# Splitting depthwise convolutions between TensorE and VectorE, and products with C between GpSimd and VectorE, in a four-layer image kernel on one core

## The chip, the core and the metric

The kernel runs on one core of a Trainium2 chip. The core has five engines that run side by side, each through its own queue of instructions in order: TensorE (PE, matrix products into the PSUM memory), VectorE (DVE, elementwise work and scans), ScalarE (ACT, functions such as exp, and copies), GpSimd (POOL, elementwise work in the SBUF memory) and SyncE (SP, which here issues DMA transfers). Engines wait for each other by semaphores. A wait at the head of a queue holds up everything behind it.

The metric is the time of one execution on the device in microseconds (us); lower is better.

## The reference

The input is eight images of 64 channels and 64 x 64 pixels in float32. Four layers follow each other:

- Layer 0: 1x1 convolution, self-attention over all 4096 pixels, a depthwise 3x3 convolution, another 1x1 convolution, added to the input.
- Layer 1: two blocks of window attention (8 x 8 pixels, 8 heads) with their MLPs.
- Layer 2: a 3x3 filter whose weights depend on place and channel, then a 1x9 convolution.
- Layer 3: a state-space scan over the pixels in four directions, and then a module that mixes four resolutions (SAFM).

Cut to what the change touches:

```python
# layer 0, after the attention; layer 3, before the scan; layer 3, at the end:
y = depthwise_conv_3x3(x, w)           # nine taps, one weight per channel and tap

# layer 3, the scan: 128 channels, 16 states, 4 directions, 4096 pixels
def step(h, inp):
    u_t, dt_t, B_t, C_t = inp
    h = h * jnp.exp(dt_t[..., None] * A) + dt_t[..., None] * B_t[:, :, None, :] * u_t[..., None]
    return (h, jnp.einsum('bkcn,bkn->bkc', h, C_t))

# layer 3, SAFM: four groups of 16 channels, pooled by 1, 2, 4 and 8
s = _dwconv3(max_pool(parts[i], 2**i), mfr_w[i], mfr_b[i])     # then repeated back to 64 x 64
out = einsum('bchw,oc->bohw', concatenate(outs), aggr_w) + aggr_b
return gelu(out) * x
```

## The kernel before, in words

Images go in pairs: 64 channels of two images fill the 128 partitions. A pair's 4096 pixels are cut into eight chunks of 512 columns (`NCH`, `CH`), one bank of PSUM each.

`tile_kernel` runs the *front* of pair 0 alone: layers 0 to 2 and the sources of the scan. Then, for each pair p, `scans` runs the scan of pair p, and beside it other work as a Python generator: the *back* of pair p - 1 (the end of layer 3 and the output) and then the front of pair p + 1. The last pair's scan has only backs beside it. Each piece of such work yields a number, its cost in the planner's units, and `scans` advances the generator after each step of the scan so that the work ends with it. The emitted program then passes a scheduler that orders the instructions of each engine. The costs that are yielded are the same before and after the change.

A scan runs through 64 units a pair (2 images, 4 directions, 8 chunks), and each unit through 8 *steps* of two states: 512 steps a pair, 2048 in all. The partitions hold 64 channels times two states. A step of `scans` works like this:

- `fetch`: two DMAs on SP's queue spread the rows of B and C to all partitions.
- `products` (L1809): GpSimd multiplies B with dt*u for both halves, 1024 columns, into `v`, which has eight buffers.
- `step`: for each half, ScalarE writes exp(dt*A) into a PSUM bank `dad` (L1831), VectorE scans (L1834), and ScalarE keeps the last column in `carries` (L1842). Then the result is multiplied by C, into `v` again (L1845, L1848).
- `sums` (L1860): TensorE adds `v` up in the PSUM bank `yd`, two or three steps later.

Who multiplies by C is decided by `own`, the number of halves that VectorE takes. During the full attention (`dense`) and for the last two images `own` is 1, and 2 in every fourth step. In all other steps it is 0 and 1 in turn. With 0, both scans write to `h` in SBUF, one copy on ScalarE keeps both carries, and one GpSimd instruction of 1024 columns multiplies both halves (L1845). With 1, the second scan overwrites its PSUM bank and VectorE multiplies it, while GpSimd multiplies the first half.

A depthwise convolution of one chunk is `taps_sum`: nine products on TensorE with diagonal matrices of the tap's weights (`spread_taps`), added in one bank (L1275), or the first n of these and the others as multiply-adds on VectorE into the same bank (L1277). Three places use it: `cacc` in layer 0 (8 chunks a pair), `xacc` in `scan_sources` (8 chunks for each image) and `pa` in `back` (8 chunks a pair). In the first two, n is 5 while the front runs alone (`self.alone`) and 9 beside a scan. In `back`, unless it runs alone at the very end, the taps are taken with the aggregation matrix scaled by the tap's weight, so that convolution and aggregation are one sum of nine products; three products for the coarser resolutions follow (L1979), and the bias is made once by a small product (`pmb`, `ab`). Alone at the end, `back` does all nine taps on VectorE (L1264, L1266, tile `sacc`), copies the result to `S`, and multiplies it with the aggregation matrix.

Of the kernel before, what the change touches and what calls it, by code (L numbers as in the profile page):

```python
# [9 lines left out]
F32 = mybir.dt.float32  # L10
AF = mybir.ActivationFunctionType
ALU = mybir.AluOpType
# [3 lines left out]
B, C, HH, WW = 8, 64, 64, 64  # L16
# [1143 lines left out]
class _Direct:  # L1160
# [127 lines left out]
    def layer0(self, p):  # L1288


        nc, tc, w, net, half = self.nc, self.tc, self.w, self.net, self.HALF
        X = self.flat("X")
        nc.sync.dma_start(X, self.net.x[2 * p : 2 * p + 2].rearrange("b c h w -> (b c) (h w)"))
        att = self.padded("att")
        VT = self.flat("VT").rearrange("p (t c) -> p t c", c=P)

        def at(rows, t):
            return X[rows, t * P : (t + 1) * P]

        with self.work("w0") as wk:  # L1300
            for g in range(8):
                pv = self.bank("pval", (P, 4, P))
                nc.tensor.matmul(pv, lhsT=net.ones[0:1, :], rhs=net.b1row.rearrange("o a c -> o (a c)").unsqueeze(1).to_broadcast([1, 4, P]), start=True, stop=False)
                for j in range(4):
                    nc.tensor.matmul(pv[:, j, :], lhsT=at(slice(0, P), 4 * g + j), rhs=net.w1bd, start=False, stop=(j == 3))
                nc.scalar.activation(VT[:, 4 * g : 4 * g + 4, :], pv, AF.Relu)
                yield 3

            parts = wk.tile([P, 2, 32, NCH], F32, name="parts", tag="parts", bufs=1)
            self.dense = 1  # L1310
            for jc in range(NCH):
                po = self.total("po")

                def weigh(t, es):
                    for im in range(2):
                        nc.tensor.matmul(  # L1316
                            po[half[im]], lhsT=VT[:, t, half[im]], rhs=es[im], start=(t == 0), stop=(t == 31)
                        )

                last = None  # L1320
                for t in range(32):
                    ss = [self.bank(f"s{im}") for im in range(2)]
                    for im in range(2):
                        nc.tensor.matmul(  # L1324
                            ss[im], lhsT=at(half[im], t), rhs=X[half[im], jc * CH : (jc + 1) * CH], start=True, stop=True
                        )
                    es = []
                    for im in range(2):
                        e = wk.tile([P, CH], F32, name="e", tag="e", bufs=5)
                        nc.scalar.activation(  # L1330
                            e, ss[im], AF.Exp, scale=C**-0.5, accum_out=parts[:, im, t, jc : jc + 1]
                        )
                        es.append(e)
                    if last is not None:
                        weigh(*last)
                    last = (t, es)
                    yield 5.8
                weigh(*last)
                nc.vector.tensor_copy(self.rows(att, jc), self.img(po))

            self.dense = 0
            sums = net.sums[:, p]
            nc.vector.tensor_reduce(sums, parts, AX.X, ALU.add)
            rec = wk.tile([P, 2, 32], F32, name="rec", tag="rec", bufs=1)
            nc.vector.reciprocal(rec, sums)
            for g in range(8):
                pr = self.bank("prec")
                for j in range(4):
                    for im in range(2):
                        nc.tensor.matmul(  # L1350
                            pr[half[im], j * P : (j + 1) * P],
                            lhsT=rec[:, im, 4 * g + j : 4 * g + j + 1].to_broadcast([P, 64]),
                            rhs=w["ident"],
                            start=True,
                            stop=True,
                        )
                d = self.rows(att, g)
                nc.vector.tensor_tensor(d, d, self.img(pr), ALU.mult)
                yield 3
        with self.work("w0b") as wk:  # L1360
            diag = self.spread_taps(wk, w["dw2"])
            for c in range(NCH):
                acc = self.bank("cacc", (P, 8, 64))
                yield from self.taps_sum(acc, diag, att, 8 * c, 1.56, wt=w["dw2"], n=5 if self.alone else TAPS)
                cv = wk.tile([P, 8, 64], F32, name="cv", tag="cv")
                nc.scalar.activation(cv, acc, AF.Relu, scale=net.bn23[:, 0:1], bias=net.bn23[:, 1:2])
                pw = self.bank("pw")
                nc.tensor.matmul(pw, lhsT=w["w3bd"], rhs=cv, start=True, stop=True)
                nc.scalar.activation(pw, pw, AF.Identity, scale=net.bn23[:, 2:3], bias=net.bn23[:, 3:4])
                x = X[:, c * CH : (c + 1) * CH]  # L1370
                nc.vector.tensor_tensor(x, x, pw, ALU.add)
                yield 2.25
        return X
# [271 lines left out]
    def scan_sources(self, p, X2):  # L1645
# [3 lines left out]
        with tc.tile_pool(name="w3", bufs=2) as wk:  # L1649
# [9 lines left out]
            for im in range(2):  # L1659
# [9 lines left out]
                XT = self.flat("XT").rearrange("p (w h) -> p h w", h=64)  # L1669
                for c in range(NCH):  # L1670
                    acc = self.bank("xacc", (P, 8, 64))
                    yield from self.taps_sum(acc, diag, pad, 8 * c, 1.5, wt=w["cw"], n=5 if self.alone else TAPS)
                    cv = wk.tile([P, 8, 64], F32, name="xcv", tag="xz")
                    nc.scalar.activation(cv, acc, AF.Silu, bias=w["cb"])
                    last = nc.scalar.activation(XT[:, 8 * c : 8 * c + 8, :], cv, AF.Copy)
                    nc.scalar.dma_start(xc[:, c * CH : (c + 1) * CH], cv.rearrange("p a b -> p (a b)"))
                    yield 1.4
# [133 lines left out]
    def step(self, i, st):  # L1811
# [5 lines left out]


        n0 = 2 * (i % 8)
        own = 1 + (i % 4 == 3) if u["image"] >= B - 2 or self.dense else i % 2  # L1820
        rev = k >= 2

        def along(t):
            return t[:, ::-1] if rev else t

        h = wk.tile([P, 2 - i % 2, TD], F32, name="hd", tag=f"h{i % 2}", bufs=2)
        hs = []
        for j in range(2):
            n = n0 + j
            da = self.bank("dad", (P, TD), "da")  # L1830
            nc.scalar.activation(da, u["du"][:, j, 0], AF.Exp, scale=net.As[:, k, n : n + 1])  # L1831
            first = 0.0 if at == 0 else self.carries[:, n : n + 1]
            to = da if j >= 2 - own else h[:, j]
            nc.vector.tensor_tensor_scan(along(to), along(da), along(v[:, j]), first, ALU.mult, ALU.add)  # L1834
            hs.append(to)
            if at < NTD - 1 and (own or j):
                ends = h[:, :, 0] if rev else h[:, :, TD - 1]
                cs = self.carries[:, n0 : n0 + 2]
                if own:
                    ends = to[:, 0:1] if rev else to[:, TD - 1 : TD]  # L1840
                    cs = self.carries[:, n : n + 1]
                nc.scalar.activation(cs, ends, AF.Copy)  # L1842

        if own == 0:
            st["w"] = nc.gpsimd.tensor_tensor(v, h, self.twice(CC), ALU.mult)  # L1845
        for j in range(2 if own else 0):
            engine = nc.vector if j >= 2 - own else nc.gpsimd
            m = engine.tensor_tensor(v[:, j], hs[j], CC, ALU.mult)  # L1848
            st.setdefault("w", m)
# [32 lines left out]
    def back(self, p):  # L1882
# [27 lines left out]
        with tc.tile_pool(name="w5", bufs=1) as wk:  # L1910
            prev, n, ups = F, 64, []
            alone = p == B // 2 - 1
            for i in range(1, 4):
# [40 lines left out]
                ups.append(up)  # L1954
                prev = pool
                yield 7
            ab = w["aggr_b"]
            if not alone:
                near = self.spread_taps(wk, w["mw"][:, 0, :], w["agT"][:, 0, :])
                pm = self.bank("pmb")  # L1960
                nc.tensor.matmul(pm[:, 0:1], lhsT=w["agT"][:, 0, :], rhs=w["mb"][:, 0:1], start=True, stop=True)
                ab = wk.tile([P, 1], F32, name="ab", tag="ab")
                nc.vector.tensor_tensor(ab, pm[:, 0:1], w["aggr_b"], ALU.add)
            for c in range(NCH):
                cols = slice(c * CH, (c + 1) * CH)
                if alone:
# [4 lines left out]
                    pa = self.bank("pa", (P, 8, 64))  # L1971
                    nc.tensor.matmul(pa, lhsT=w["agT"][:, 0, :], rhs=S, start=True, stop=False)
                else:
                    pa = self.bank("pa", (P, 8, 64))
                    yield from self.taps_sum(pa, near, F, 8 * c, 1.5, stop=False)
                for i in range(1, 4):
                    k = 2**i
                    r = 8 // k
# [4 lines left out]
                        start=False,  # L1983
                        stop=(i == 3),
                    )
                last = nc.scalar.activation(pa, pa, AF.Gelu, bias=ab)
                nc.vector.tensor_tensor(pa, pa, self.rows(F, c), ALU.mult)
                nc.vector.tensor_tensor(X[:, cols], X[:, cols], pa.rearrange("p a b -> p (a b)"), ALU.add)
                nc.sync.dma_start(out[:, cols], X[:, cols])
# [53 lines left out]
```

## Time and profile before

Three runs took 11924.33, 11923.68 and 11909.1 us: the median is 11923.68 us. The profiled execution took 11912.44 us, with a span of 11910.6 us from its first to its last instruction.

| | PE | DVE | ACT | POOL |
|---|---|---|---|---|
| busy, us | 9941.2 | 7896.1 | 6958.5 | 7344.5 |
| share of the span | 83% | 66% | 58% | 62% |

The weight loads of TensorE (PEld, 3381.8 us) lie beside its products. TensorE's mean granted clock is 0.904 of full speed.

| from - to, us | what runs |
|---|---|
| 0 - 1561 | front of pair 0, alone |
| 1561 - 2595 | scan 0, beside the full attention of pair 1 |
| 2595 - 4158 | scan 0, beside the rest of the front of pair 1 |
| 4158 - 7008 | scan 1, beside the back of pair 0 and the front of pair 2 |
| 7008 - 9859 | scan 2, beside the back of pair 1 and the front of pair 3 |
| 9859 - 11911 | scan 3, beside the back of pair 2; the back of pair 3 at the end |

How to read the lines quoted below: times are in us, means in ns. L1848 is line 1848 of the kernel before; `vd<-hd,C` is what an instruction writes and reads; `128x512 f32` is 128 partitions times 512 columns of float32; x404 is how often. A float32 product appears as two rows of matmul. Matmuls are pipelined and the end of each is modelled, so the distance of their starts tells more than their length. "Idle before" is idle time of the engine before such instructions, with what ended most of it.

### The profile page before, as it was taken

The page shows a single profiled execution, that of the slowest core. Times are in us where ns is not written, and L with a number is a line of the kernel's source. Part 1 is how long each engine was busy: PE and PEld are TensorE (multiplying, and loading weights), DVE is VectorE, ACT ScalarE, POOL GpSimd, SP SyncE. Part 2 cuts the span into 40 slices and gives each one's busy share as a digit, 9 for nine tenths or more (in the row PEclk, how much of TensorE's full clock was granted, in tenths as well). Part 3 has the DMA queues.
Part 4 walks back from the last instruction along what each step waited for, and adds up shares of the span by engine and source line. Part 5 has one row for each costly group of instructions (what it writes and reads, how often), then busy time and mean ns, then how long its engine had stood idle before and what let it go on. Part 6 is the DMA issues. An engine that isn't in the chain of part 4 may idle for free. (4 is left out here: it accounts for less than half of the span.)

```text
span 11910.6 us, 161652 instructions
## 1 busy us (share of the span) xinstructions
PE 9941.2 (83%) x56180; PEld 3381.8 (28%) x56180; DVE 7896.1 (66%) x9071; ACT 6958.5 (58%) x16089; POOL 7344.5 (62%) x3799
## 2 busy tenths in 40 slices
PE   9987999998889779999888968999888886665565
PEld 2244332223332223223342313222333221111111
DVE  0033368876776475876766564777676648989998
ACT  5555367766664555775665554777566355555554
POOL 0000068876777574776756673777676658889994
PEclk9998999999999889999999979999999987786768
DMA  0000055554444453554433453555343346666663
GB/s 20 1 2 2 33 168 174 172 159 120 125 131 125 152 158 111 169 170 133 132 107 110 141 177 96 157 167 173 115 132 114 109 149 190 182 191 199 207 204 119
DMA packets 779774, 1577.05 MB, mean 132 GB/s; under 512 B 89280, under 2 KB 89408, under 8 KB 778176
## 3 DMA queue, kind: packets, MB, share of 16 engines
q1 hardware_dynamic: 736320, 1443.18, 39.9%
q10 hardware_dynamic: 42624, 123.44, 3.7%
q8 instruction: 444, 7.27, 0.3%
q14 instruction: 386, 3.16, 0.1%
HBM read 1197.16 MB, written 100.66 MB: 109 GB/s over the span
## 5 line engine op out<-in xcount | busy, mean ns | idle before, releaser
L1809 POOL TENSOR_TENSOR vd<-B,du 128x1024 f32<-128x1024 f32 x2048 | 4791.4, 2359 | 2982.0 <-DMA B<-rows 1733.3
L1860 PE MATMUL yd<-vd,pack 128*64 128x512 f32 x8192 | 2707.2, 690 | 637.7 <-POOL vd L1848 505.3
L1831 ACT ACTIVATE dad<-du,As 128x512 f32<-128x512 f32 x4096 | 2716.3, 682 | 708.8 <-DVE hd L1834 330.4
L1834 DVE TENSOR_TENSOR_SCAN hd<-dad,carry,vd 128x512 f32<-128x512 f32 x1874 | 2355.3, 1270 | 529.3 <-ACT dad L1831 400.0
L1834 DVE TENSOR_TENSOR_SCAN dad<-dad,carry,vd 128x512 f32<-128x512 f32 x1710 | 2153.0, 1277 | 186.4 <-ACT dad L1831 183.4
L1848 POOL TENSOR_TENSOR vd<-hd,C 128x512 f32<-128x512 f32 x1333 | 1698.1, 1278 | 651.6 <-DVE hd L1834 648.5
L1324 PE MATMUL s<-X 64*128 64x512 f32 x4096 | 1539.3, 646 | 75.4 <-ACT e L1330 66.8
L1330 ACT ACTIVATE e<-s 128x512 f32<-128x512 f32 x2048 | 1196.3, 588 | 483.7 <-PE s L1324 483.4
L1845 POOL TENSOR_TENSOR vd<-hd,C 128x1024 f32<-128x1024 f32 x404 | 952.2, 2357 | 794.2 <-issue 393.6
L1848 DVE TENSOR_TENSOR vd<-dad,C 128x512 f32<-128x512 f32 x1955 | 1296.6, 676 | 148.5 <-ACT carry L1842 115.1
L1860 PEld LDWEIGHTS yd<-vd,pack 128*64 128x64 f32 x8192 | 643.2, 151 | 2319.1 <-issue 1129.8
L1316 PE MATMUL po<-e,VT 128*64 128x512 f32 x4096 | 1259.4, 622 | 5.8 <-ACT e L1330 5.0
L1324 PEld LDWEIGHTS s<-X 64*128 64x128 f32 x4096 | 421.8, 186 | 1178.7 <-issue 832.5
L1842 ACT ACTIVATE carry<-dad 128x1 f32<-128x1 f32 x1707 | 286.4, 169 | 760.2 <-DVE dad L1834 656.7
L1842 ACT ACTIVATE carry<-hd 128x1 f32<-128x1 f32 (+1 forms) x1521 | 302.0, 200 | 625.2 <-DVE hd L1834 611.5
L1483 PE MATMUL w_av<-wide,vals 64*32 64x64 f32 x16384 | 490.7, 225 | 117.9 <-DVE w_oc L1512 74.6
L1316 PEld LDWEIGHTS po<-e,VT 128*64 128x64 f32 x4096 | 249.6, 135 | 833.7 <-issue 569.4
L1471 ACT ACTIVATE wide<-wide 128x512 f32<-128x512 f32 x512 | 310.7, 628 | 289.4 <-DVE wide L1470 289.2
L1483 PEld LDWEIGHTS w_av<-wide,vals 64*32 64x32 f32 x16384 | 402.7, 111 | 257.1 <-issue 138.1
L1834 DVE TENSOR_TENSOR_SCAN hd<-dad,vd 128x512 f32<-128x512 f32 x267 | 319.9, 1211 | 225.6 <-POOL vd L1809 189.0
L1494 PE MATMUL w_av<-wide,each 64*32 64x128 f32 x8192 | 463.2, 280 | 5.6 <-issue 5.4
L1243 PE MATMUL pv<-n_sq,pack 128*128 128x512 f32 x576 | 345.5, 683 | 143.9 <-ACT n_sq L1241 133.3
(259 smaller groups left out, 11257.1 us busy)
## 6 DMA issues: line engine op xcount, KB each, us to landing
B<-rows SPq DMA_DIRECT2D x2048, 256.0 KB, 3.6
C<-rows SPq DMA_DIRECT2D x2048, 256.0 KB, 3.5
du<-du SPq DMA_DIRECT2D x384, 512.0 KB, 5.6
du<-du ACTq DMA_DIRECT2D x128, 512.0 KB, 5.1
xs<-xt SPq DMA_DIRECT2D x128, 256.0 KB, 3.7
xs<-xc SPq DMA_DIRECT2D x128, 256.0 KB, 3.8
xc<-xcv ACTq DMA_DIRECT2D x64, 256.0 KB, 2.0
xt<-XT ACTq DMA_DIRECT2D x32, 512.0 KB, 4.8
```

Source lines behind the costliest of these rows:

```text
L1316: nc.tensor.matmul(po[half[im]], lhsT=VT[:, t, half[im]], rhs=es[im], start=(t == 0), stop=(t == 31))
L1324: nc.tensor.matmul(ss[im], lhsT=at(half[im], t), rhs=X[half[im], jc * CH : (jc + 1) * CH], start=True, stop=True)
L1330: nc.scalar.activation(e, ss[im], AF.Exp, scale=C**-0.5, accum_out=parts[:, im, t, jc : jc + 1])
L1483: nc.tensor.matmul(self.av[rows, 0, x % 4 + j], lhsT=net.vals[half[im], x + j, 4 * g + h], rhs=es[g][half[im], j, h], tile_position=(64 * ...
L1494: nc.tensor.matmul(self.av[rows, 1, x % 4 : x % 4 + 2], lhsT=net.each[half[im], 32 - HD - HD * h : 64 - HD - HD * h], rhs=es[g][half[im], ...
L1809: self.nc.gpsimd.tensor_tensor(v, self.twice(st["B"]), self.units[i // 8]["du"][:, :, 1], ALU.mult)
L1831: nc.scalar.activation(da, u["du"][:, j, 0], AF.Exp, scale=net.As[:, k, n : n + 1])
L1834: nc.vector.tensor_tensor_scan(along(to), along(da), along(v[:, j]), first, ALU.mult, ALU.add)
L1842: nc.scalar.activation(cs, ends, AF.Copy)
L1845: st["w"] = nc.gpsimd.tensor_tensor(v, h, self.twice(CC), ALU.mult)
L1848: m = engine.tensor_tensor(v[:, j], hs[j], CC, ALU.mult)
L1860: m = nc.tensor.matmul(u["y"][self.HALF[j]], lhsT=w["fold"], rhs=st["v"][:, j], start=(i % 8 == 0), stop=(i % 8 == 7))
```

## The change

It has three parts. The fronts that run beside a scan now split `cacc` and `xacc` as the front that runs alone does: five taps on TensorE, four on VectorE. In `step`, `own` is never 0: outside the attention and the last two images every step gives one half to GpSimd and one to VectorE, so the single instruction for both halves and the shared carry copy go away, and `h` is one tile of 512 columns with four buffers in place of two tags. In `back`, unless it runs alone, four taps are done by VectorE into `S`, a quarter of `big` with one buffer, to which the bias is added; one product with the aggregation matrix brings `S` into the sum, and five taps remain as products. The small bias product goes away.

```diff
@@ layer0
-                yield from self.taps_sum(acc, diag, att, 8 * c, 1.56, wt=w["dw2"], n=5 if self.alone else TAPS)
+                yield from self.taps_sum(acc, diag, att, 8 * c, 1.56, wt=w["dw2"], n=5)
@@ scan_sources
-                    yield from self.taps_sum(acc, diag, pad, 8 * c, 1.5, wt=w["cw"], n=5 if self.alone else TAPS)
+                    yield from self.taps_sum(acc, diag, pad, 8 * c, 1.5, wt=w["cw"], n=5)
@@ step
-        own = 1 + (i % 4 == 3) if u["image"] >= B - 2 or self.dense else i % 2
+        own = 1 + (i % 4 == 3 and (u["image"] >= B - 2 or self.dense))
...
-        h = wk.tile([P, 2 - i % 2, TD], F32, name="hd", tag=f"h{i % 2}", bufs=2)
+        h = wk.tile([P, TD], F32, name="hd", tag="h", bufs=4)
...
-            to = da if j >= 2 - own else h[:, j]
+            to = da if j >= 2 - own else h
...
-            if at < NTD - 1 and (own or j):
-                ends = h[:, :, 0] if rev else h[:, :, TD - 1]
-                cs = self.carries[:, n0 : n0 + 2]
-                if own:
-                    ends = to[:, 0:1] if rev else to[:, TD - 1 : TD]
-                    cs = self.carries[:, n : n + 1]
-                nc.scalar.activation(cs, ends, AF.Copy)
-
-        if own == 0:
-            st["w"] = nc.gpsimd.tensor_tensor(v, h, self.twice(CC), ALU.mult)
-        for j in range(2 if own else 0):
+            if at < NTD - 1:
+                ends = to[:, 0:1] if rev else to[:, TD - 1 : TD]
+                nc.scalar.activation(self.carries[:, n : n + 1], ends, AF.Copy)
+
+        for j in range(2):
@@ back
-            ab = w["aggr_b"]
             if not alone:
                 near = self.spread_taps(wk, w["mw"][:, 0, :], w["agT"][:, 0, :])
-                pm = self.bank("pmb")
-                nc.tensor.matmul(pm[:, 0:1], lhsT=w["agT"][:, 0, :], rhs=w["mb"][:, 0:1], start=True, stop=True)
-                ab = wk.tile([P, 1], F32, name="ab", tag="ab")
-                nc.vector.tensor_tensor(ab, pm[:, 0:1], w["aggr_b"], ALU.add)
...
+                    S = self.img(self.share(big, 3))
                     pa = self.bank("pa", (P, 8, 64))
-                    yield from self.taps_sum(pa, near, F, 8 * c, 1.5, stop=False)
+                    for t in range(TAPS):
+                        tap = F[:, 8 * c + t // 3 : 8 * c + t // 3 + 8, t % 3 : t % 3 + 64]
+                        wt = w["mw"][:, 0, t : t + 1]
+                        if t == 0:
+                            nc.vector.tensor_scalar(S, tap, wt, w["mb"][:, 0:1], ALU.mult, ALU.add)
+                        elif t < 4:
+                            nc.vector.scalar_tensor_tensor(S, tap, wt, S, ALU.mult, ALU.add)
+                        else:
+                            nc.tensor.matmul(pa, lhsT=near[:, t], rhs=tap, start=(t == 4), stop=False)
+                        if t % 3 == 2:
+                            yield 1.5
+                    nc.tensor.matmul(pa, lhsT=w["agT"][:, 0, :], rhs=S, start=False, stop=False)
...
-                last = nc.scalar.activation(pa, pa, AF.Gelu, bias=ab)
+                last = nc.scalar.activation(pa, pa, AF.Gelu, bias=w["aggr_b"])
```

## The prediction

> **What bounds the kernel now.** I went from the summary of engine shares to the busy time by stretch, because no engine is busy through the whole span (TensorE 83%, VectorE 66%, GpSimd 62%), and a share of the whole hides which engine stops which stage. The table of stretches covers one image pair from the end of its attention (2595 us) to the end of its scan (4158 us), and then the first half of the output stage beside the next scan. Columns: length, then busy time and instruction count of TensorE (PE), weight loads, VectorE (DVE), ScalarE (ACT), GpSimd (POOL), then granted clock and DMA.
>
> ```profile
> core 0: us, PE busy (x) PEld busy (x) DVE busy (x) ACT busy (x) POOL busy (x), PEclk, DMA share, GB/s
> 2595.00:2798.00 203.00, 176.59 (x847) 65.81 (x851) 119.43 (x135) 104.56 (x222) 132.82 (x67) 0.92 0.40 120
> 2798.00:2976.00 178.00, 155.87 (x2743) 77.43 (x2732) 131.46 (x161) 111.40 (x233) 127.60 (x62) 0.95 0.41 121
> 2976.00:3127.00 151.00, 117.85 (x1186) 43.09 (x1186) 113.08 (x127) 106.38 (x203) 127.93 (x64) 0.90 0.50 146
> 3127.00:3347.00 220.00, 183.97 (x3158) 93.75 (x3157) 158.05 (x205) 139.51 (x283) 134.51 (x66) 0.96 0.36 106
> 3347.00:3505.00 158.00, 125.38 (x1214) 47.19 (x1213) 120.65 (x152) 114.61 (x217) 128.03 (x64) 0.93 0.48 141
> 3505.00:3723.00 218.00, 186.79 (x515) 63.26 (x516) 149.02 (x175) 89.72 (x178) 131.74 (x65) 0.93 0.37 111
> 3723.00:3906.00 183.00, 169.99 (x436) 57.41 (x435) 115.48 (x129) 105.19 (x202) 131.09 (x64) 1.00 0.45 135
> 3906.00:4158.00 252.00, 192.21 (x432) 62.69 (x430) 107.36 (x112) 133.16 (x216) 138.24 (x68) 0.82 0.51 159
> 4158.00:4288.00 130.00, 93.24 (x198) 22.85 (x196) 103.65 (x108) 77.80 (x168) 126.61 (x62) 0.82 0.65 199
> ```
>
> Each of these rows holds about 32 scan steps. With no front beside them, 32 steps take 109 us (192 steps in the 656 us from 10862 us on) to 130; the rows with depthwise convolutions (the first, seventh and eighth) take 183 to 252. The ninth row is GpSimd's: 126.6 of 130 us. The narrower stretches below show why convolutions are so dear: one group of eight convolution chunks in the scan sources, one of the output stage, and the output stage of pair 2, which runs beside the last scan.
>
> ```profile
> 3963.00:4038.00 75.00, 75.00 (x181) 29.36 (x180) 21.25 (x20) 32.58 (x51) 32.57 (x16) 0.98 0.24 76
> 4423.00:4506.00 83.00, 83.00 (x193) 36.53 (x194) 9.71 (x14) 7.76 (x15) 8.15 (x5) 1.00 0.08 29
> 10399.00:10552.00 153.00, 138.86 (x352) 45.04 (x352) 129.32 (x143) 104.81 (x208) 122.39 (x67) 0.97 0.60 181
> ```
>
> In the first two TensorE never stops, and VectorE works 21 and 10 us of them: the scan all but stands. In the third, VectorE is busy 85% and TensorE 91%. The timeline of TensorE inside the first shows the turn of a chunk; the two lines after it are from the front that runs alone at the start, which already splits the nine taps five and four.
>
> ```profile
> 3989.96 8.00 PE L1275 MATMUL xacc<-XI,diag 128*128 128x512 f32 x18
> 3997.88 1.08 PE L1860 MATMUL yd<-vd,pack 128*64 128x512 f32 x4
> 3998.89 7.99 PE L1275 MATMUL xacc<-XI,diag 128*128 128x512 f32 x18
> ...
> 1486.10 14.43 PE L1275 MATMUL xacc<-XI,diag 128*128 128x512 f32 x33
> 1489.04 3.13 DVE L1277 SCALAR_TENSOR_TENSOR xacc<-XI,pack,xacc 128x512 f32<-128x512 f32 x4 [31.73 <-PE xacc L1275]
> ```
>
> A tap is two rows of matmul here: 18 rows in 7.99 us is 0.444 us a row, 0.888 us a tap, and a chunk comes every 8.9 us with one step's sums between. The busy mean of a row (592 ns) overlaps the next, so I do not use it. Four taps on VectorE take 3.13 us. The costliest groups give the products with C:
>
> ```profile
> L1848 POOL TENSOR_TENSOR vd<-hd,C 128x512 f32<-128x512 f32 x1333 | 1698.1, 1278 | 651.6 <-DVE hd L1834 648.5
> L1845 POOL TENSOR_TENSOR vd<-hd,C 128x1024 f32<-128x1024 f32 x404 | 952.2, 2357 | 794.2 <-issue 393.6
> L1848 DVE TENSOR_TENSOR vd<-dad,C 128x512 f32<-128x512 f32 x1955 | 1296.6, 676 | 148.5 <-ACT carry L1842 115.1
> ```
>
> **Part 1, convolutions of the fronts.** Three fronts run beside a scan, each with 8 chunks of cacc and 16 of xacc: 72 chunks. Each loses four taps on TensorE (3.55 us) and gains four on VectorE (the tile's 0.756 us each, 3.02 us). Per pair: TensorE -85 us, VectorE +73 us. The four taps stand behind the chunk's five matmuls, and the scan's operations queue behind them on VectorE; in the changed program's order the next chunk's five taps stand before or beside them on TensorE, with a step's sums between, so the two engines can overlap. About 6 to 7 steps stand inside a group of eight xacc chunks, and 23 inside cacc's, by the scans on VectorE there.
>
> **Part 2, products with C.** The 404 steps that gave both products to GpSimd (2.357 us) now give it one (1.278) and VectorE the other (0.676). For 32 steps, some 15 to 17 of these: GpSimd -16 to -18 us, VectorE +10 to +12. Their one carry copy becomes two, 356 more on ScalarE at 0.17 to 0.20 us, 65 us in all over stages where ScalarE is at 41 to 73%: nothing, as long as scans and not copies end its waits. The second scan result now sits in a PSUM bank until VectorE has multiplied it, 0.7 us longer; nothing while VectorE is not full, up to 0.7 us a step if it is.
>
> **Part 3, output stage.** Per chunk nine taps become five, plus one product of S with the aggregation weights: three tap-times less, 2.66 us on TensorE. VectorE gets four taps with S in SBUF; the nearest rows are the alone output stage's (0.810 us for the first, 0.751 for the others), 3.06 us a chunk. Below 0.67 (the lightest full tile here) or above 0.81 I see no reason for. S has one buffer, so the next chunk's taps wait for S's product; three up-sampled products and five taps (8 x 0.888 = 7.1 us) lie beside them. Two bursts stand alone, and one lies in the last scan. The bias product and its addition go away: nothing.
>
> **Sum for the stretches of a pair.** I take the busiest engine of each row before and after.
> Row 1: TensorE 176.6 becomes 148; VectorE 119.4 + 24.2 + 10 = 154, the new maximum: -23.
> Row 2: TensorE 155.9 stays (VectorE 142).
> Row 3: GpSimd 127.9 becomes 112, VectorE 123: -5.
> Row 4: TensorE 184 stays (VectorE 169).
> Row 5: GpSimd 128 becomes 112, VectorE 131: +3.
> Row 6: TensorE 187 stays (VectorE 160).
> Row 7: 5.3 chunks of the first xacc group lie here; TensorE 170 - 19 = 151, VectorE 142: -19.
> Row 8: the other 10.7; TensorE 192.2 - 38 = 154, VectorE 107.4 + 32.3 + 12.2 = 152: -38.
> Together -82. Rows 1, 7 and 8 end with two engines within 6 us of each other, where each waits for the other now and then; I take off a quarter: -60 a pair, -180 for three.
> Row 9, beside two scans: GpSimd 126.6 - 16 = 110, VectorE 114: -13 each, -25.
> The two bursts of the output stage: TensorE 83 - 8 x 2.66 = 62, VectorE 9.7 + 24.5 = 34: -21 each, -43. The changed order also lays 11 steps' scans between these taps; I count no gain from that.
> The last scan's burst: VectorE 129 + 24.5 = 154 against TensorE 139 before: +15 to +24, I take +20, since that stage is VectorE's on both sides.
> The attention and the tail of the last scan keep their split. Sum: -180 - 25 - 43 + 20 = -228.
>
> [...] The clock columns are 0.98 and 1.00 in the dense bursts and 0.82 where TensorE has gaps. [...] But less TensorE work must cost some clock in stages that TensorE bounds, rows 2, 4 and 6 (527 us a pair, 1580 in three): 0.01 of clock is 17 us there. I allow 0.016, +28 us. So -200 us.
>
> The profiled execution took 11912.4 us (span 11910.6); 11912 - 200 = **11712 us**. The median of the three runs, 11923.7, lies 0.1% above that execution, inside the noise I allow for.
>
> **Rivals.**
> *Larger gain.* The waits shrink with the busiest engine: -82 x 1563/1321 = -97 a pair, -290; and the 22 steps laid into the two output bursts come free, at 4.1 us each (row 9, 130/32) -90. With -25 - 43 + 20: -428, 11480 us. For it: the scan stands still in those bursts. Against: the scan's sums are not in TensorE's order there, and its v buffers are eight. Chance 0.17.
> *The freed time is given back.* The extra VectorE product of part 2 lands wholly on the path in rows 2 to 6 (10.5 us each, 158 in three pairs), since window attention and the scan share VectorE's queue. -200 + 158 = -42, 11870 us. For it: VectorE at 0.68 to 0.76 there; against: TensorE or GpSimd is busier in each. Chance 0.18.
> *Slower: convolution chunks in lock-step.* If a bank, or the order of sums, makes TensorE wait for the chunk's taps on VectorE, and these for the scan ahead of them, a chunk takes 4.44 + 3.13 + 1.08 + 3.22 (two scans of 1.27 and one product) = 11.9 us instead of 8.9. That is +3.0 x 72 = +216, and the 180 of gain is gone: -200 + 180 + 216 = +196, 12108 us. It decides from about 9.2 us a chunk (20 us left over 72 chunks). [...] Against: the alone front keeps 4.3 us a chunk. Chance 0.25.
>
> **Numbers.** The forecast has 0.40. Its own range is 11610 to 11810. A difference below 0.2% (24 us) can't be told from none. Faster: 0.40 + 0.17 + part of the second rival, 0.65; same 0.07; slower 0.28. With 0.28 on the slow side the range has to enter it: 11530 to 12040.
>
> **What would show it.** xacc groups of 75 us fall to 50 to 60 with VectorE over 40 us; rows of matmul stay 0.44 us apart. Row 9's stretch falls to about 118. Output bursts take under 75 us. The last scan's output stage grows by about 20. The forecast is wrong if a chunk comes at over 9 us, if window attention lengthens by over 10 us a row, or if the clock falls below 0.88 in the rows of one pair.

## The result, and the profile after

The changed kernel took 11724.1 us (median of 4 runs, 11719.74 to 11727.07), against 11920.7 us for the kernel before (4 runs): a ratio of 0.9836, with a 95% interval of 0.9819 to 0.9853. That is 197 us less; the forecast was 200. The profiled execution took 11724.67 us, its span is 11722.8 us, and the granted clock is 0.896 (before: 0.904).

The right total hides terms that were wrong in both directions, so the stages come first. I cut both traces at the same events: the first and last product of the full attention, the last product of a convolution group, and the first product with B of a scan and of its steps. Each cell is the length of a stretch in us, with the scan steps in it in brackets.

| stretch | pair 0 before | pair 0 after | pair 1 before | pair 1 after | pair 2 before | pair 2 after |
|---|---|---|---|---|---|---|
| first 32 steps of the scan | | | 130.3 (32) | 125.6 (32) | 130.3 (32) | 125.3 (32) |
| then to the attention's start | | | 248.7 (32) | 208.8 (30) | 248.6 (32) | 203.0 (30) |
| attention | 1031.8 (255) | 1027.8 (255) | 943.8 (212) | 954.7 (214) | 947.6 (212) | 952.7 (214) |
| to the end of the cacc group | 116.6 (16) | 127.5 (29) | 104.7 (13) | 118.4 (27) | 104.7 (13) | 118.7 (27) |
| to the start of the xacc groups | 1131.4 (200) | 1110.8 (187) | 1121.4 (189) | 1094.7 (175) | 1118.3 (189) | 1101.7 (175) |
| xacc groups | 181.0 (19) | 136.8 (19) | 178.2 (18) | 139.5 (17) | 178.1 (18) | 141.2 (17) |
| to the next scan | 119.8 (16) | 123.3 (16) | 122.6 (16) | 127.5 (17) | 123.8 (16) | 129.3 (17) |

In the last scan, steps 128 to 256 went from 501.6 to 533.1 us; its other parts moved by less than 3 us. Executions differ by some 10 us in a long stretch whose instructions are the same (the 1110.8 us of pair 0 are 1099 in the trace of `keep_last`, below), so only differences that repeat over the pairs are read below.

The profile gives the same cuts with the columns of the first table of the prediction. Before, for pair 0 from the end of the attention to the end of the xacc groups, for pair 1 from step 32 to the attention, and for steps 128 to 256 of the last scan:

```profile
2609.00:2726.00 117.00, 105.46 (x349) 41.85 (x348) 55.64 (x61) 41.07 (x89) 68.28 (x35) 0.97 0.36 105
2726.00:3857.00 1131.00, 951.78 (x9586) 383.89 (x9586) 828.85 (x994) 696.47 (x1388) 816.40 (x398) 0.94 0.43 127
3857.00:4038.00 181.00, 176.69 (x409) 67.21 (x408) 53.33 (x54) 98.17 (x146) 77.47 (x38) 0.93 0.37 117
4288.00:4537.00 249.00, 208.03 (x517) 85.43 (x514) 144.67 (x172) 101.53 (x224) 112.49 (x59) 0.88 0.41 124
10360.00:10862.00 502.00, 329.69 (x804) 88.02 (x806) 434.51 (x472) 286.90 (x627) 415.64 (x226) 0.79 0.63 189
```

After, for the same stretches, with the stretch from the xacc groups to the next scan (fourth row) and the first 32 steps of scan 1 (fifth row) between them:

```profile
2602.00:2730.00 128.00, 99.19 (x347) 37.11 (x348) 117.88 (x138) 66.94 (x158) 105.83 (x61) 0.87 0.56 167
2730.00:3841.00 1111.00, 935.68 (x9525) 390.16 (x9522) 843.19 (x1052) 678.85 (x1410) 664.35 (x372) 0.93 0.41 121
3841.00:3978.00 137.00, 123.65 (x278) 41.87 (x276) 102.70 (x126) 108.37 (x161) 68.93 (x39) 0.86 0.48 151
3978.00:4101.00 123.00, 68.50 (x135) 14.96 (x134) 76.96 (x87) 69.31 (x121) 64.49 (x39) 0.70 0.61 190
4101.00:4226.00 125.00, 93.35 (x200) 23.65 (x202) 112.69 (x125) 82.26 (x189) 110.98 (x62) 0.85 0.72 217
4226.00:4435.00 209.00, 176.97 (x460) 71.22 (x456) 146.26 (x183) 96.93 (x209) 100.64 (x52) 0.89 0.40 124
10142.00:10675.00 533.00, 324.40 (x752) 83.00 (x754) 478.36 (x500) 288.37 (x628) 421.82 (x225) 0.77 0.58 177
```

In the first row VectorE is now full (118 of 128 us, before 56 of 117); in the fifth VectorE has taken GpSimd's place (113 against 111 us); in the last VectorE, the busiest engine there before and after, is busy 478 of 533 us. The groups of the products with C on the page after (in the changed kernel they stand in L1842, and the sums in L1854):

```profile
L1842 POOL TENSOR_TENSOR vd<-hd,C 128x512 f32<-128x512 f32 x1737 | 2210.8, 1278 | 1765.4 <-DVE hd L1834 1719.2
L1842 DVE TENSOR_TENSOR vd<-dad,C 128x512 f32<-128x512 f32 x2359 | 1559.6, 673 | 167.9 <-ACT carry L1838 128.7
```

The 404 products moved at the sizes that the rows before gave. GpSimd now waits for the scan far longer (1719 us before this group, 649 us before its group of one half in the kernel before), and the execution is shorter all the same.

The turn of a chunk in an xacc group after the change, from the timeline of TensorE:

```profile
3933.55 4.56 PE L1275 MATMUL xacc<-XI,diag 128*128 128x512 f32 x10
3938.04 1.08 PE L1854 MATMUL yd<-vd,pack 128*64 128x512 f32 x4
3939.05 4.56 PE L1275 MATMUL xacc<-XI,diag 128*128 128x512 f32 x10
...
3950.91 4.56 PE L1275 MATMUL xacc<-XI,diag 128*128 128x512 f32 x10
3955.40 1.08 PE L1854 MATMUL yd<-vd,pack 128*64 128x512 f32 x4
3956.41 4.13 PE L1275 MATMUL xacc<-XI,diag 128*128 128x512 f32 x9
```

And from the timeline of VectorE, within the same chunks:

```profile
3952.31 0.68 DVE L1842 TENSOR_TENSOR vd<-dad,C 128x512 f32<-128x512 f32 x1
3952.91 0.74 DVE L1277 SCALAR_TENSOR_TENSOR xacc<-XI,pack,xacc 128x512 f32<-128x512 f32 x1
3953.56 0.68 DVE L1842 TENSOR_TENSOR vd<-dad,C 128x512 f32<-128x512 f32 x1
3954.16 0.74 DVE L1277 SCALAR_TENSOR_TENSOR xacc<-XI,pack,xacc 128x512 f32<-128x512 f32 x1
3954.82 1.27 DVE L1834 TENSOR_TENSOR_SCAN hd<-dad,carry,vd 128x512 f32<-128x512 f32 x1
```

A chunk comes every 5.5 us (3933.55, 3939.05) where it came every 8.9, or after 6.4 us where the sums of two steps stand between (in the lines left out). TensorE goes from taps to sums to taps without a gap, and VectorE puts taps, scans and products one behind the other: in these lines neither waits for the other's chunk. The starts of VectorE's taps and products lie 0.60 to 0.66 us apart, less than the 0.68 to 0.74 us that each lasts.

### The profile page after: what moved, and what is told of

Its sections match the earlier page's. It is cut to its first block, busy times and chain, and to the rows that moved or that the text cites. A ratio compares the mean times of both kernels' runs of the same rounds, so it can differ in the third digit from the quotient of the medians.

```text
span 11722.8 us, 161838 instructions
## 1 busy us (share of the span) xinstructions
PE 9682.2 (83%) x55454; PEld 3278.2 (28%) x55454; DVE 8416.8 (72%) x9856; ACT 7078.9 (60%) x16513; POOL 6924.2 (59%) x3799
## 5 line engine op out<-in xcount | busy, mean ns | idle before, releaser
L1842 POOL TENSOR_TENSOR vd<-hd,C 128x512 f32<-128x512 f32 x1737 | 2210.8, 1278 | 1765.4 <-DVE hd L1834 1719.2
L1854 PE MATMUL yd<-vd,pack 128*64 128x512 f32 x8192 | 2684.9, 691 | 602.0 <-POOL vd L1842 501.5
L1834 DVE TENSOR_TENSOR_SCAN dad<-dad,carry,vd 128x512 f32<-128x512 f32 x2064 | 2602.0, 1275 | 228.4 <-ACT dad L1831 224.8
L1834 DVE TENSOR_TENSOR_SCAN hd<-dad,carry,vd 128x512 f32<-128x512 f32 x1520 | 1922.7, 1266 | 347.5 <-ACT dad L1831 298.2
L1842 DVE TENSOR_TENSOR vd<-dad,C 128x512 f32<-128x512 f32 x2359 | 1559.6, 673 | 167.9 <-ACT carry L1838 128.7
L1854 PEld LDWEIGHTS yd<-vd,pack 128*64 128x64 f32 x8192 | 651.9, 151 | 2292.6 <-issue 1169.1
L1838 ACT ACTIVATE carry<-dad 128x1 f32<-128x1 f32 x2063 | 345.8, 169 | 903.4 <-DVE dad L1834 804.4
L1838 ACT ACTIVATE carry<-hd 128x1 f32<-128x1 f32 x1521 | 303.1, 200 | 678.4 <-DVE hd L1834 669.8
L1771 PE MATMUL pdd<-xs,xdt 128*128 128x512 f32 x512 | 343.7, 758 | 122.3 <-DVE hd L1834 64.2
L1330 ACT ACTIVATION_READ_ACCUMULATOR e<-s 128x1 f32 x2048 | 406.7, 199 | 0.0
```

What stands on the lines that cost most here:

```text
L1330: nc.scalar.activation(e, ss[im], AF.Exp, scale=C**-0.5, accum_out=parts[:, im, t, jc : jc + 1])
L1838: nc.scalar.activation(self.carries[:, n : n + 1], ends, AF.Copy)
L1854: m = nc.tensor.matmul(u["y"][self.HALF[j]], lhsT=w["fold"], rhs=st["v"][:, j], start=(i % 8 == 0), stop=(i % 8 == 7))
```

## The experiments

All ratios are to the kernel before, on the same chip in the same session. The kernel before itself had medians of 11919.4 us in the session of the first four runs, 11910.3 in that of the next four and 11913.7 in the last, so differences between kernels of different sessions are given by the medians and by the ratios where they differ.

**Each part alone: p1_fronts.**

```diff
 kernel before:
-  n=5 if self.alone else TAPS
+  n=5                                   # cacc and xacc; products and output stage as before
```

> The kernel before with only the fronts' convolutions split five and four. Theory A (TensorE was the wall inside the convolution groups, and the products matter little): most of the gain is here, 130 to 180 us, ratio to before 0.985 to 0.989; xacc groups fall from 74 us to 42 to 50. Theory B (the whole gains because GpSimd is relieved): 30 to 60 us, 0.995 to 0.9975, with the groups shorter but the time given back right behind them while GpSimd catches up. Theory C (the parts need each other, since the scan laid beside the taps is then GpSimd's): under 30 us.

Measured: 11798.8 us, ratio 0.9903 (0.9887 to 0.9918), 121 us less than the before of its session. Below theory A, far above B and C. Its stretches for pair 0, from the end of the attention to the next scan:

```profile
2608.00:2753.00 145.00, 106.78 (x374) 36.99 (x372) 124.56 (x139) 75.41 (x167) 137.88 (x69) 0.85 0.57 167
2753.00:3858.00 1105.00, 921.46 (x9500) 381.01 (x9500) 782.26 (x949) 663.91 (x1311) 747.40 (x365) 0.94 0.40 119
3858.00:3994.00 136.00, 124.23 (x276) 42.47 (x276) 93.91 (x112) 106.06 (x148) 76.99 (x38) 0.85 0.46 149
3994.00:4119.00 125.00, 66.58 (x145) 15.25 (x143) 71.77 (x77) 69.91 (x119) 76.01 (x39) 0.70 0.61 191
```

The xacc groups shrink from 181 to 136 us with the same 19 steps: the gain is theirs. The cacc group does not shrink, it grows, from 117 to 145 us, with GpSimd full (138 of 145). The scheduler has laid 34 steps beside it instead of 16. The stretch behind has 18 steps less, and shortens by only 27 us. A step beside the cacc group cost more than it saved beside the window attention: there 18 steps less are 26 us less, 1.5 us each, and TensorE is busy 921 of 1105 us where it was 952 of 1131. So the two xacc groups of a pair pay about 44 us, and the cacc group, in this run, next to nothing.

**p2_products.** The kernel before with the changed `step`:

```diff
-  own = 1 + (i % 4 == 3) if u["image"] >= B - 2 or self.dense else i % 2
+  own = 1 + (i % 4 == 3 and (u["image"] >= B - 2 or self.dense))
```

> The kernel before with only the new split of the products with C. Theory A: 10 to 40 us faster (0.997 to 0.999), from the GpSimd-bound stretch at the start of scans 1 and 2, with TensorE as full as before in the convolution groups. Theory B: 80 to 130 us faster (0.989 to 0.993), spread over all stages outside the attention. A third possibility, that VectorE's extra 273 us show in window attention: slower by 20 to 100 us.

Measured: 11846.1 us, ratio 0.9941 (0.9927 to 0.9955), 73 us less: between theories A and B. Its stretches at the start of scan 1:

```profile
4142.00:4268.00 126.00, 94.66 (x203) 23.82 (x204) 113.50 (x125) 82.59 (x189) 111.17 (x62) 0.85 0.70 215
4268.00:4488.00 220.00, 190.32 (x507) 76.47 (x504) 125.51 (x152) 91.21 (x204) 100.05 (x52) 0.92 0.39 118
```

The first 32 steps, where GpSimd was full, fell from 130.3 to 126.5 us in scan 1, and did not fall in scan 2 (131.6): VectorE fills with 113.5 us as GpSimd empties. The next stretch fell from 249 to 220 and 224 us. Its output burst still takes 82.7 us of TensorE, but 12 scans now lie inside it where there were none; before the burst there are 38 instead of 54, behind it 4 instead of 12, and the other 12 have moved into the attention (+12 and +11 us, 430 scans instead of 418). So at the start of a scan, what I had booked as GpSimd's relief is mostly a matter of where the steps lie. Part of the gain is spread, though: with as many steps as before, the three cacc groups are 11 us shorter together, and the three stretches from the xacc groups to the next scan 21 us.

**p3_back.** The kernel before with the changed output stage.

> The kernel before with only the new output stage. Theory A: the two bursts beside scans 1 and 2 fall from 83 to 60 to 66 us (-35 to -60 together with steps laid into them), the last scan's output stage grows by 15 to 30 us; in all 10 to 40 us faster, 0.9965 to 0.999. If the burst's steps come free (the rival of a larger gain) it is 60 to 100 us faster.

Measured: 11889.2 us, ratio 0.9977 (0.9967 to 0.9987), 30 us less. The bursts fell from 82.7 to 63.5 us each with 10 scans laid into them, and the last scan grew (steps 128 to 256: 529.1 us). Theory A holds in each of its parts.

The three alone give -121, -73 and -30: -224 together, 27 us more than the whole. One place where they do not add is the stretches before the next scan: part 2 alone took 21 us off them, but in the whole they are only 3.5 us shorter than with part 1 alone.

**p13_no_products.** The changed kernel with the old `step`.

> The changed kernel with the old split of the products (own is 0 and 1 in turn). Theory A: 150 to 200 us faster than before, 0.983 to 0.9875, within 40 us of the changed kernel. Theory B: 60 to 100 us faster at most, so 100 us or more behind the changed kernel. Theory C: no more than 50 us faster than before.

Measured: 11778.7 us, ratio 0.9888 (0.9872 to 0.9904). Parts 1 and 3 add (121 and 30 against 141), and theory C falls. The 141 us lie below theory A's 150 too. The products are worth 55 us on top of them by the medians (11778.7 - 11724.1), 62 by the ratios: more than theory A's 40, less than B's 100.

**own_early.** Where do these 55 us lie? The new split of the products only in the first 80 steps of scans 1 and 2:

```diff
 p13_no_products:
-  own = 1 + (i % 4 == 3) if u["image"] >= B - 2 or self.dense else i % 2
+  own = 1 + (i % 4 == 3) if u["image"] >= B - 2 or self.dense else i % 2 if i >= 80 or u["image"] < 2 else 1
```

> The changed kernel with the new split of the products in the first 80 steps of scans 1 and 2 alone, the old one elsewhere. Theory: the products pay where the output stage and the start of the front meet a scan that GpSimd feeds, so 25 to 45 of the 55 us between the changed kernel and the one with the old products come back: 11735 to 11755 us. Rival: they pay a little in every stage, then no more than 10 us come back (11770 us and over). If the late steps were harmed by the new split, it is faster than the changed kernel.

Measured: 11739.4 us, ratio 0.9857 (0.9842 to 0.9872): by the medians 39 of the 55 us come back, by the ratios 60% of the distance (0.9888 to 0.9836), as the theory has it. From step 32 to the attention its stretches take 200.2 and 203.2 us, about as in the changed kernel; with the old products it is 231.2 and 230.8. Not all of this is won: there are 30 steps instead of 37 in them, and the attention, which takes the other seven, is 12 us longer. Of the 404 double products 370 are still there; splitting these is worth the other 30 to 40%.

**cacc9.** Does the cacc group pay? The changed kernel with nine taps on TensorE there, beside a scan:

```diff
-  yield from self.taps_sum(acc, diag, att, 8 * c, 1.56, wt=w["dw2"], n=5)
+  yield from self.taps_sum(acc, diag, att, 8 * c, 1.56, wt=w["dw2"], n=5 if self.alone else TAPS)
```

> The changed kernel with nine taps on TensorE in layer 0's convolution alone, beside a scan. Theory A2 (in this group the time freed on TensorE is filled by scan steps that cost nothing later, beside window attention): within 20 us of the changed kernel; from the end of the attention to the end of the group some 105 to 115 us with 13 to 16 steps, and the stretch up to the next convolutions about 20 to 25 us longer. Theory A as predicted (each chunk pays 3.55 us less VectorE's share, 17 to 23 us a pair): 50 to 70 us slower than the changed kernel.

Measured: 11750.5 us, ratio 0.9868 (0.9853 to 0.9883). By the medians it is 26 us slower than the changed kernel, by the ratios 38: between theory A2's 20 and the 50 to 70 of the forecast's own step, and neither holds as written. The stretches do what A2 says: 112.9, 102.1 and 102.1 us to the end of the group with 16, 12 and 12 steps, then 1128.9, 1121.8 and 1121.5 us with 200, 189 and 189 steps. Together they are 18 us longer than after the change, and 41 us longer than in the trace of `keep_last` below, whose fronts are those of the changed kernel. So the group does pay, but some 20 to 40 us in three pairs, a quarter to a half of what its chunks save on TensorE (8 x 3.55 = 28 us a pair).

**n7_fronts.** Seven taps on TensorE and two on VectorE in both groups (`n=5 if self.alone else 7`).

> The changed kernel with seven taps on TensorE and two on VectorE in the fronts beside a scan. Theory A (TensorE is still the wall in the xacc groups): each group grows from 44 to 57 to 59 us (8 x 2 x 0.888 = 14.2), 75 to 90 us over six groups, layer 0's group gives little either way; 60 to 95 us slower than the changed kernel. If VectorE had become the wall at five and four: equal or faster.

Measured: 11735.9 us, ratio 0.9853 (0.9838 to 0.9868): only 12 us slower than five and four by the medians, 20 by the ratios, whose intervals overlap, and below the 60 expected. But not because VectorE is the wall in the xacc groups. One of them in this run, and the same one in the changed kernel:

```profile
3927.00:3989.00 62.00, 62.00 (x149) 23.46 (x148) 34.18 (x39) 34.33 (x57) 28.82 (x16) 0.96 0.38 123
```

```profile
3934.00:3977.00 43.00, 43.00 (x112) 15.98 (x111) 41.41 (x52) 36.27 (x55) 28.73 (x16) 1.00 0.53 164
```

With seven taps TensorE is busy all of 62 us and VectorE 34; with five, TensorE all of 43 and VectorE 41. The six groups are 14.5 to 18 us dearer each, 97 us together, a little more than the two taps cost on TensorE (14.2 each), and five and four is where both engines are full. By the trace, the rest gave this back: the gaps between the two groups of a pair (32 us in three pairs), the cacc groups (each 8 us shorter, with 2 to 4 steps fewer beside it), the stretches behind those, which did not get longer (1100.8, 1091.8, 1088.8 us), and those before the next scan (16 us). My expectation had left all of these as they were; that was wrong.

**keep_last.** The changed kernel with the old output stage where it runs beside the last scan.

```diff
+  last_scan = p == B // 2 - 2
...
+  elif last_scan:
+      pa = self.bank("pa", (P, 8, 64))
+      yield from self.taps_sum(pa, near, F, 8 * c, 1.5, stop=False)
   else:
       S = self.img(self.share(big, 3))
```

> The changed kernel with the old output stage in the last scan alone. The last scan is bound by VectorE, so the 24.5 us of taps should all come back: 25 to 35 us faster than the changed kernel (11690 to 11700 us), steps 128 to 256 of that scan back from 533 to about 502 us. If the growth there comes from something else of the change (the new order, or the copies of the carries): no change.

Measured: 11694.1 us, ratio 0.9817 (0.9804 to 0.9831): 30 us less than the changed kernel by the medians, 23 by the ratios. Steps 128 to 256 of the last scan in its profile:

```profile
10139.00:10637.00 498.00, 338.76 (x804) 88.41 (x806) 433.64 (x472) 286.96 (x627) 415.34 (x225) 0.78 0.63 191
```

VectorE is busy 434 us there instead of 478, and the stretch takes 498 us instead of 533: most of what VectorE is spared comes off the time. It is spared 45 us, though, and not the 24.5 that I had summed for the taps: in this stage they took twice as long (see the last section).

**mixed and mixed_pa5: a version that beats both.** keep_last with seven and two taps in the cacc group; then with five taps of the output stage on VectorE instead of four beside scans 1 and 2.

```diff
 mixed:      cacc: n=5 if self.alone else 7
 mixed_pa5:  -  elif t < 4:
             +  elif t < 5:
```

> The changed kernel with seven and two taps in layer 0's group, five and four in the xacc groups, and the old output stage in the last scan. If the stages add: 30 us from the last scan, and some 20 to 50 us from layer 0's group, which seven taps shortened in the run with seven everywhere: 11640 to 11675 us, ratio to before 0.978 to 0.981. If that shortening was a run's noise, or the steps taken out of the group cost as much later: 11685 to 11700 us, as with the old output stage alone.

> As the mixed kernel, with five taps of the output stage on VectorE and four on TensorE beside scans 1 and 2. TensorE is still the wall of these two bursts (63 of 66 us, VectorE 47), so each should fall by about 7 us (8 x 0.888) to 58 to 60 us: 8 to 15 us faster than the mixed kernel. If the one buffer of S has become the limit, the burst stays at 65 us or grows.

Measured: mixed 11670.6 us, ratio 0.9792 (0.9779 to 0.9806); mixed_pa5 11664.3 us, ratio 0.9786 (0.9772 to 0.9799). The first gains 24 us over keep_last by the medians, 30 by the ratios, inside its range; the two intervals just touch. The traces do not place this gain. In mixed the cacc groups are 6.5 to 9 us shorter than in keep_last, but the stretches behind them 5 to 11 us longer. Both together, over three pairs, take 3691 us with nine taps (cacc9), 3674 and 3650 with five (the changed kernel, keep_last) and 3624, 3653 and 3637 with seven (n7_fronts, mixed, mixed_pa5): a trend, but traces with the same split lie as far apart as the splits.

In the second the burst fell from 65.4 to 60.3 us:

```profile
4339.00:4400.00 61.00, 56.36 (x129) 24.28 (x130) 51.50 (x70) 30.64 (x51) 6.86 (x5) 1.00 0.30 92
```

TensorE and VectorE are now near each other there (56 and 52 of 61 us), so I would expect little of a sixth tap. The 6 us over mixed are less than the 8 expected, and the two intervals overlap: the burst is shorter by the trace, the whole is not shown to be.

## Why the prediction was right, point by point

**TensorE was the wall of the xacc groups.** Right in mechanism: the groups fell from 72 to 75 us to 42 to 46, no new wait took its place (5.5 us a chunk, against 4.44 + 1.08 from the rows), and n7_fronts gives the cost of taps put back. The stretch of both groups lost 44, 39 and 37 us a pair, against the 57 that rows 7 and 8 gave, and 43 after a quarter was taken off.

**Row 1, the cacc group: -23 a pair.** This step failed. Part 1 names 23 steps inside this group, but row 1 kept the steps of before. The freed time was filled with 13 or 14 steps that the scheduler took from the window attention: +11 to +14 us in the group, -17 to -27 behind it. An estimate from these numbers: the taps free 28 us of TensorE, and the group still grew, so a step cost about 3 us in it and had cost 1.2 to 1.9 us where it came from. The clock may have a share: in pair 0's group it fell from 0.97 to 0.87, and with nine taps put back (cacc9) it is 0.97 again; no run separates it from the steps. By cacc9 the group pays 6 us a pair (stretches) to 13 (ratios); by p1_fronts alone next to nothing. Rows 1 to 8 came to -131 us over three pairs and not -180.

**Part 2 in row 9: -13 for each scan.** Mis-sized: -5 each, and the stretch takes 125 us, not the 118 named as a sign. VectorE, which I put at 114 us, was at 113, but a stretch in which two engines stand at 113 and 111 us takes 125. The products paid instead in the stretch behind, and beside the cacc group.

**Output bursts: -21 each, and no gain from steps laid into them.** Too small. TensorE's part fell about as computed (83 to 65 us, 62 summed), and 12 scans lie in the burst. The stretch to the attention lost 40 and 46 us, of which 11 and 5 came back in the attention, which carries 12 scans more. p3_back and p2_products share this gain: with the new products alone, 12 scans lie in a burst of the old length. It is part of the rival of a larger gain, which put 11 steps into a burst; 6 steps is what the trace shows.

**Last scan: +20.** Mis-sized: +31 there, and 23 to 30 by keep_last. The forecast took 24.5 us for the 32 taps, and saw no reason for one below 0.67 or above 0.81 us. They took 50.1 us, because 23 of them stood until an instruction of GpSimd had ended (last section). That the term missed by 11 us and not by more is no merit of the sum: the time that the taps take on VectorE was off by 25 us.

**Clock: +28.** The 0.016 behind it was an estimate of mine, and no run isolates it: over the whole execution the clock went from 0.904 to 0.896. The stretch with the window attention had 0.94 of the clock before, 0.93 after. In pair 0's xacc groups TensorE has no gaps (busy 43.0 of 43 us in each) and the clock is 1.00; in its cacc group it fell from 0.97 to 0.87, and behind the xacc groups, where TensorE is busy 69 of 123 us (before 65 of 120), from 0.72 to 0.70. A clock below 0.88 in the rows of a pair was named as a sign of being wrong. It shows, but row 8 stood at 0.82 before the change, so this sign could tell nothing.

**Against the rivals.** The lock-step of chunks is refuted by the timeline. VectorE's products did not lengthen the window attention: in p2_products, with as many steps as before, the stretch that holds it is 0 to 5 us longer (1131.7, 1122.2, 1123.2), where this rival needs some 52. Time was given back in another way and place, in the cacc group.

Sum of the terms as they turned out: -131 (fronts) - 10 (row 9) - 85 (to the attention) + 12 (attentions) + 30 (last scan) = -184, of the spans' -188. Before its allowance for the clock the forecast had -228. The fronts fell 49 us short and the last scan 10, the start of the scans gave 15 us more, and the 28 us set aside for the clock, which no trace shows as such, cover most of what was missing. The main mechanism was right; that the total came within 3 us is luck.

What stays open: why seven taps should serve the cacc group better than five, and whether they do, is not shown stage by stage; an order that keeps the steps out of the group at five taps was not tried.

## What to carry to other kernels

When a stretch has one engine at 100% and another nearly idle, compare the queue's pace (distance of starts) and not the busy time, and move work until both are full; here that was five taps and four. Then ask what the scheduler will put into the time you free: work pulled in from a stretch where it was mostly hidden pays little, and the same split can be right in one place (xacc, 37 to 44 us a pair), worth much less in the next (cacc, 6 to 13 us a pair), and taps moved to an engine that is the bound are a loss (the last scan, 31 us). A duration taken from a stage where the neighbour is idle need not hold where it is busy: the same taps cost 22 us a burst and 50 us in the last scan. Count the effect by stage, with the units of the other work in each stage beside the time, or errors of tens of us in both directions will pass as one right number.

## What the hardware showed that I had not expected

**The taps from SBUF to SBUF stood still while GpSimd worked.** The taps of the output stage read and write SBUF alone. In the two bursts, where GpSimd is busy 6.6 and 6.2 of 66 us, the 32 taps take 22 us each time. In the last scan, where GpSimd is busy 422 of 533 us, they take 50.1 us:

```profile
L1969 DVE TENSOR_SCALAR big<-F,pack x8: 521/1872/2644, 10129.9 to 10334.4; 128x512 f32<-128x512 f32 x8
L1971 DVE SCALAR_TENSOR_TENSOR big<-F,pack,big x24: 717/1634/3492, 10131.4 to 10354.1; 128x512 f32<-128x512 f32 x24
```

The columns are minimum, median and maximum in ns. Two of the taps, and the instructions of GpSimd at the same time:

```profile
10225.19 2.23 DVE L1971 SCALAR_TENSOR_TENSOR big<-F,pack,big 128x512 f32<-128x512 f32 x1
10231.49 2.50 DVE L1971 SCALAR_TENSOR_TENSOR big<-F,pack,big 128x512 f32<-128x512 f32 x1
```

```profile
10224.08 2.79 POOL L1809 TENSOR_TENSOR vd<-B,du 128x1024 f32<-128x1024 f32 x1
10231.09 2.34 POOL L1809 TENSOR_TENSOR vd<-B,du 128x1024 f32<-128x1024 f32 x1
```

GpSimd ends at 10226.87 and 10233.43, the taps at 10227.42 and 10233.99: 0.55 and 0.56 us later. So it is with the 23 taps of the last scan that started while an instruction of GpSimd ran: 21 end 0.55 us after it (0.28 to 0.29 for the first tap of a chunk), however long it ran, and the other two, of 3.49 and 2.64 us, end 0.55 and 0.29 us after the next one. The other nine took 0.52 to 0.75 us. The taps of xacc, which read and write a PSUM bank, show nothing of the kind: 88 of them started while GpSimd ran, and none took over 0.756 us. That the place of the operands makes this difference is read from these groups; no run moved the same taps.

**One tensor, SBUF to SBUF.** The first tap of the output stage, a multiply and add of one tensor from SBUF to SBUF, took 0.52 to 0.55 us in the 15 of 24 cases where no instruction of GpSimd ran as it started, a third less than the row I took for it, which writes to PSUM (0.810 us):

```profile
L1969 DVE TENSOR_SCALAR big<-F,pack x24: 518/546/2644, 4307.2 to 10334.4; 128x512 f32<-128x512 f32 x24
```

```profile
L1971 DVE SCALAR_TENSOR_TENSOR big<-F,pack,big x72: 717/751/3492, 4308.2 to 10354.1; 128x512 f32<-128x512 f32 x72
```

The taps with two tensors have a median of 751 ns, the same as those into PSUM where the output stage runs alone (L1264 of the kernel before, 751 ns). What makes the first tap cheaper is not shown.

**Starts and ends.** In the lines of VectorE quoted for the turn of a chunk, each instruction starts 0.08 to 0.09 us before the one ahead has ended. Between scans and products a tap so costs some 0.65 us of the queue there, not the 0.756 that I summed; in the front that runs alone, taps of one chunk that follow each other directly start 0.78 to 0.79 us apart (3.13 us for four).
